# Second causal attention: exponentials turned in 32x32 squares on VectorE and moved through DRAM, instead of turned 128x128 on TensorE

## The chip, the core and the metric

The kernel runs on one core of one Trainium2 chip. A core has a matrix engine (TensorE, PE in the profile, with its weight loads as PEld), three engines for elementwise work (VectorE = DVE, ScalarE = ACT, GpSimd = POOL), and queues that start transfers (SP's queue carries nearly all of them here). Each engine works through its own instructions in order and waits on semaphores for the others. The metric is the device time of one execution in microseconds (us): the median of several runs, 882.38 us before the change.

## What is computed

The reference is a decoder of two layers on 8 sequences of 128 tokens with 512 features, in float32. Each layer is a self attention, a second attention over a context, and a feed-forward part; each part is added to the residual and normalized over the features. The change lies in the second layer's self attention:

```python
qkv = jnp.clip(jnp.einsum('bsd,ed->bse', hidden_states, Wqkv), -8, 8)
q, k, v = jnp.split(qkv, [512, 1024], axis=-1)
q = _layer_norm(q, q_ln_w, q_ln_b); k = _layer_norm(k, k_ln_w, k_ln_b)
# 32 heads of 16 features
scores = jnp.einsum('bqhd,bkhd->bhqk', q, k) * scale + slopes * (key_pos - query_pos)
scores = jnp.where(causal, scores, -1e30)
probs = jax.nn.softmax(scores, axis=-1)
out = jnp.einsum('bhqk,bkhd->bqhd', probs, v)          # then @ Wout, + x, layer norm
```

## The kernel before

**The stage.** The second layer's self attention is a loop over 8 batches (sequences), `for b in range(B)`, and in it over `f in (0, 2)`: two units of 16 heads each, 16 units in all. I name a unit by (b, f) and call f = 0 the even and f = 2 the odd unit. Around the loop's units run the projections of the next batch and the output projection of the last one:

- even unit: scores of the unit, then `normed(0, b + 1)` (queries of the next batch: four matmuls, clip to +-8, layer norm over rows) and `normed(1, b + 1)` (keys, the same, and on POOL a product with and a sum of the norm's weights, L669 and L670);
- odd unit: scores of the unit, `turned_queries` (the next queries are turned by TensorE, L691, and copied with scale and bias by ACT), `values`, `turned_tokens` of batch b + 2, `projection` of batch b - 1 (8 matmul records, in two halves), and `turned_keys` (the keys turned by TensorE, L701, and multiplied by DVE into `kbd`, two copies with the other head of each pair zeroed, L703).

**A unit (class Heads16).** TensorE writes the scores into two double banks of PSUM (L165; the pool of double banks, `ps2`, has two). DVE adds the bias, negates and takes the row minimum, head by head: 16 instructions of L184 that write the tile `e` (two buffers). ACT takes the exponential in place with the row sum (`exps`, L197), 16 instructions. `divide` takes the reciprocals (DVE, L208) and multiplies the exponentials (POOL, L211). `turn` has TensorE turn `e` in twelve 128x128 transposes (L228) through the same double banks, and DVE and ACT each copy half of the result to SBUF as `pT` (L229). `out` multiplies the turned probabilities with the values (L247, L253), and DVE copies the result into `oT` (L259). A unit is turned in the following unit and its `out` is made in the one after that.

**What sets the order.** Instructions are recorded in program order, and a scheduler may move them; a few places pin it with `tc.issue_after`. `late` and `keys_late` hold norms that are pushed behind the heads of the next unit. Single banks of PSUM (`ps1`, four) are handed out in turn to the projections, the turned pieces and `out`. After the loop come pieces of the following attention (`front.go`), whose weights `w_X_...` are loaded on SP's queue while this stage runs.

**The helper of the norms.** `moments` is three instructions on DVE (statistics L91, aggregate L93, variance plus epsilon L95) and a power on POOL (L97); the row norm itself is one instruction of DVE (L107, L667).

Of the kernel before, what the change touches and what calls it, by code (L numbers as in the profile page):

```python
# [13 lines left out]
ALU = mybir.AluOpType  # L14
# [29 lines left out]
def decoder(ctx: ExitStack, tc: tile.TileContext, a: dict, out: bass.AP):  # L44
# [69 lines left out]

    late = []
# [30 lines left out]
    class Heads16:  # L146
# [11 lines left out]
        def __init__(self, pool, units, bias, o_dst, name, between=()):  # L158
            self.pool, self.units, self.o_dst, self.name, self.rc = pool, units, o_dst, name, None
            s = [banks(f"s_{name}_{i}") for i in range(2)]  # L160
# [9 lines left out]
            self.e = pool.tile([P, 4, self.W], F32, tag="e", name=f"e_{name}", bufs=2)  # L170
            self.m = sm.tile([P, 2, 4, 2], F32, tag="m", name=f"m_{name}")
            self.su = sm.tile([P, 2, 4, 2], F32, tag="su_a", name=f"su_{name}")
            for i in range(2):
                if i and between:
                    while between:
                        with tc.issue_after(self.scored.ins):
                            self.scored = between.pop(0)()
                with tc.issue_after(self.scored.ins) if i else nullcontext():
                    for part in range(2):
                        for r in (2 * i, 2 * i + 1):  # L180
                            for x in range(2):
                                w = P >> part
                                cols = slice(2 * P * part + w * x, 2 * P * part + w * x + w)
                                self.scored = nc.vector.tensor_tensor_reduce(  # L184
                                    self.e[:, r, cols], s[i][:, r % 2, cols], bias(r, cols), -1.0, 3e38,
                                    ALU.add, ALU.min, self.m[:, part, r, x : x + 1],
                                )
# [4 lines left out]
        def exps(self, half):  # L192
            for part in range(2):
                e = self.by_heads(part)
                for r in (2 * half, 2 * half + 1):
                    for x in range(2):
                        nc.scalar.activation(  # L197
                            e[:, r, x, :], e[:, r, x, :], AF.Exp, scale=-1.0,
# [13 lines left out]

        def turn(self):


            if self.rc is None:
# [3 lines left out]
                rb = self.pool.tile([P, 2, 8, HD], F32, tag="rb", name=f"rb_{self.name}", bufs=1)  # L220
                nc.gpsimd.tensor_copy(rb, bc(rc.rearrange("p (a h) -> p a h", a=2).unsqueeze(3), [P, 2, 8, HD]))
            self.pT = self.pool.tile([P, 4, self.W], F32, tag="pT", name=f"pT_{self.name}", bufs=1)
# [14 lines left out]
            self.rT = self.pool.tile([P, 2, P], F32, tag="rT", name=f"rT_{self.name}", bufs=1)  # L237
            nc.scalar.copy(self.rT, pr[:, : 2 * P].rearrange("p (a q) -> p a q", a=2))

        def out(self):  # L240
            o = bank(f"o_{self.name}")
            for u, (_, _, v, vd) in enumerate(self.units):
                v, vd = (t() if callable(t) else t for t in (v, vd))
                late = slice(u * P + 64, u * P + P)
                for x in range(2):
                    for r in range(4):
# [3 lines left out]
                            rhs=self.pT[:, r, x * P + 64 * u : x * P + 64 * u + 64], start=(x == 0), stop=(x == 1),  # L250
                        )
                for r in range(4):
# [3 lines left out]
                        rhs=self.pT[:, r, 2 * P + 64 * u : 2 * P + 64 * u + 64], start=True, stop=True,  # L256
                    )
            if self.rc is not None:
# [7 lines left out]
            )  # L266

# [25 lines left out]
    idle = ap.tile([P, 4, 3 * P], F32, tag="e", name="idle").rearrange("p r k -> p (r k)")[:, :512]  # L293
# [355 lines left out]
    v_bufs = [values_tiles(qp, i) for i in range(2)]  # L649
# [6 lines left out]
    def normed(i, b, xT, later=None):  # L656


        n, w = (("q", w1q), ("k", w1k))[i]
        pq = bank(f"p{n}1_{b}")  # L660
        mm_acc(pq, [(xT[:, c, :], w[:, c, :]) for c in range(NC)])
        q = qp.tile([P, D], F32, tag=n, name=f"{n}1_{b}")
        nc.vector.tensor_scalar(q, pq, 8.0, -8.0, ALU.min, ALU.max)
        mean, rs = moments(q, f"{n}1_{b}")

        def normalized():
# [180 lines left out]
    for b in range(B):  # L847
# [3 lines left out]
        for f in (0, 2):  # L851
# [11 lines left out]
            if turned:  # L863
                turned.out()
# [533 lines left out]
```

## Time and profile before

| what | value |
|---|---|
| median of the runs shown | 882.38 us (880.0 to 883.82) |
| the profiled execution's own time | 883.9 us |
| its span | 882.1 us |
| granted TensorE clock, mean | 0.994 |
| busy: PE, DVE, ACT, POOL | 853.1, 545.8, 369.3, 188.5 us |
| first score matmul of the stage | at 325.30 us |
| first matmul after the stage's last projection | at 510.31 us |
| first heads instruction of unit (1,0), (7,0), (7,2) | at 349.10, 482.75, 490.19 us |
| one steady batch (two units) | 22.14 us |

How to read the profile: one execution is recorded, and every instruction has a start, a duration and what it waited for. A group names line, engine, operation, output and inputs, how often, busy time, mean duration in ns, and the idle time of its engine just before it with what ended that. The windows view gives busy time by engine in a stretch of time. The chain is the work that ended last, followed back from the end of the program, or, between two times, in order of time. The timeline lists the instructions by start. Instructions of one engine overlap a little: the start of the next one comes before the end of the last, so a chain of them is priced here from start to start.

### The profile page before, as it was taken

What the parts mean: (1) busy time and instruction counts of PE and PEld (TensorE: products, weight loads), DVE (VectorE), ACT (ScalarE), POOL (GpSimd) and SP (SyncE); (2) the same over time, 40 slices, a digit from 0 to 9 for tenths busy, and PEclk for the clock granted to TensorE, in tenths of its full rate; (3) what the DMA queues carried; (4) which work ended last, traced back from release to release, by engine and by line L of the source; (5) the groups of instructions that cost most, each with busy time, mean ns of one, the idle gap of its engine ahead of it and who ended that gap; (6) DMA issues with size and microseconds to landing.
All of it is one profiled execution on the core that took longest, in us unless ns stands there. A gap on an engine that the chain in (4) does not pass through costs nothing.

```text
span 882.1 us, 17898 instructions
## 1 busy us (share of the span) xinstructions
PE 853.1 (97%) x6482; PEld 529.9 (60%) x6482; DVE 545.8 (62%) x2166; ACT 369.3 (42%) x1535; POOL 188.5 (21%) x267
## 2 busy tenths in 40 slices
PE   9999999999899999999999999999999999999996
PEld 5766655655455455555555687758475846576454
DVE  3656787777869567777778622735363545467654
ACT  3877564754222136666666503213122322224310
POOL 2500223133333314555555300000000000000000
PEclk9999999999999999999999999999999999999999
DMA  8700000130300002000004010331213211313340
GB/s 327 306 2 26 1 14 13 49 108 1 144 13 24 1 1 97 2 1 2 2 2 145 27 72 1 75 88 42 48 37 85 44 47 37 83 43 76 81 97 36
DMA packets 30073, 50.73 MB, mean 58 GB/s; under 512 B 5536, under 2 KB 22048, under 8 KB 28192
## 3 DMA queue, kind: packets, MB, share of 16 engines
q1 hardware_dynamic: 27424, 47.49, 17.9%
q10 hardware_dynamic: 2560, 2.10, 1.1%
q8 instruction: 51, 0.84, 0.4%
q14 instruction: 38, 0.31, 0.1%
HBM read 30.69 MB, written 2.10 MB: 37 GB/s over the span
## 4 chain that ended last, share of the span: by engine, by line
PE 72%; DVE 17%; ACT 6%; POOL 2%; issue 1%; DMA 1%; SPq 0%; ACTq 0%; POOLq 0%; DVEq 0%
PE pqx L86 9%; PE pox L994 7%; PE pv L86 5%; PE pkx L86 4%; PE pvx L86 4%; PE s_x L932 4%; PE o_x L977 4%; PE pq L86 4%; PE pk L86 3%; PE po L711 3%; ACT e_a L197 3%; DVE e_a L184 3%; PE pt_a L228 3%; PE pof L618 2%; PE s_a L165 2%; PE po L86 2%
## 5 line engine op out<-in xcount | busy, mean ns | idle before, releaser
L197 ACT ACTIVATE e_a<-e_a,m_a 128x128 f32<-128x128 f32 (+1 forms) x512 | 184.8, 365 | 100.2 <-DVE m_a L184 100.2
L953 ACT ACTIVATE e_x<-s_x,m_x 128x256 f32<-128x256 f32 x128 | 58.6, 483 | 140.0 <-DVE m_x L943 132.1
L197 ACT ACTIVATION_READ_ACCUMULATOR e_a<-e_a,m_a 128x1 f32 x512 | 97.6, 191 | 0.0
L86 PE MATMUL pqx<-xTx,w_X_q 128*128 128x256 f32 x384 | 84.9, 380 | 0.0
L86 PEld LDWEIGHTS pqx<-xTx,w_X_q 128*128 128x128 f32 x384 | 72.6, 190 | 11.4 <-issue 1.8
L994 PE MATMUL pox<-w_X_o,oTx 128*128 128x512 f32 x168 | 74.1, 596 | 0.7 <-DVE oTx L983 0.6
L942 DVE TENSOR_REDUCE m_x<-s_x 128x4 f32<-128x1024 f32 x32 | 37.6, 1218 | 41.2 <-PE s_x L932 41.2
L97 POOL TENSOR_TENSOR rs_x<-ve_x,neghalf 128x1 f32<-128x1 f32 x7 | 3.8, 548 | 268.8 <-DVE ve_x L95 249.8
L211 POOL TENSOR_TENSOR e_a<-e_a,rc_a 128x512 f32<-128x512 f32 (+1 forms) x64 | 52.7, 845 | 34.9 <-DVE rc_a L208 19.3
L994 PEld LDWEIGHTS pox<-w_X_o,oTx 128*128 128x128 f32 x168 | 31.3, 190 | 40.9 <-issue 39.2
L932 PE MATMUL s_x<-kTx,qTx 32*128 32x256 f32 x768 | 50.0, 385 | 1.2 <-ACT e_x L953 1.1
L228 PE MATMUL pt_a<-ident,e_a 128*128 128x128 f32 x384 | 48.0, 273 | 2.7 <-DVE m_a L184 2.7
L228 PEld LDWEIGHTS pt_a<-ident,e_a 128*128 128x128 f32 x384 | 43.6, 140 | 11.1 <-issue 5.0
L184 DVE CUSTOM_DVE_ANT_0 e_a<-s_a,masks 128x128 f32<-128x128 f32 (+1 forms) x256 | 47.1, 252 | 4.5 <-PE s_a L165 3.2
L932 PEld LDWEIGHTS s_x<-kTx,qTx 32*128 32x128 f32 x768 | 39.0, 184 | 17.4 <-issue 11.7
L184 DVE CUSTOM_DVE_ANT_0 e_a<-s_a,alibi 128x128 f32<-128x128 f32 (+1 forms) x256 | 47.4, 253 | 2.2 <-PE s_a L165 1.3
L977 PE MATMUL o_x<-pT_x,vx 128*32 128x512 f32 x384 | 43.7, 595 | 1.9 <-issue 0.7
L184 DVE DVE_READ_ACCUMULATOR2_ANT m_a<- 128x1 f32 x512 | 42.4, 83 | 0.1
L961 DVE STREAM_TRANSPOSE e_x<-e_x 128x1024 f32<-128x1024 f32 x32 | 39.7, 1241 | 0.8
L960 DVE TENSOR_SCALAR e_x<-e_x,rc_x 128x256 f32<-128x256 f32 x128 | 36.3, 347 | 3.9 <-DVE rc_x L957 2.2
L165 PEld LDWEIGHTS s_a<-kbd,qT 32*64 32x64 f32 x1024 | 20.7, 131 | 28.5 <-issue 15.4
L103 DVE TENSOR_TENSOR x_x<-pox,x_a 128x512 f32<-128x512 f32 x7 | 4.8, 686 | 52.5 <-PE pox L994 52.5
(236 smaller groups left out, 1627.1 us busy)
## 6 DMA issues: line engine op xcount, KB each, us to landing
pT_x<-e_x SPq DMA_DIRECT2D x224, 64.0 KB, 2.0
w_X_q<-in_X_q SPq DMA_DIRECT2D x3, 1024.0 KB, 4.8
w_X_o<-in_X_o SPq DMA_DIRECT2D x3, 1024.0 KB, 4.7
w_L_Wv<-in_L_Wv SPq DMA_DIRECT2D x2, 1024.0 KB, 7.3
w_L_Wo<-in_L_Wo SPq DMA_DIRECT2D x2, 1024.0 KB, 8.0
x_in<-in_x SPq DMA_DIRECT2D x8, 256.0 KB, 8.5
ct<-in_ctx SPq DMA_DIRECT2D x8, 256.0 KB, 2.6
cT<-in_ctxT SPq DMA_DIRECT2D x4, 512.0 KB, 3.8
```

What stands on the lines that cost most here:

```text
L86: nc.tensor.matmul(ps, lhsT=l, rhs=r, start=(i == 0), stop=(i == n - 1))
L165: nc.tensor.matmul(s[r // 2][64 * u : 64 * u + 64, r % 2, cols], lhsT=qT[rows, 64 - 64 * part : P - 64 * part], rhs=kbd[rows, :, :keys], s ...
L184: self.scored = nc.vector.tensor_tensor_reduce(self.e[:, r, cols], s[i][:, r % 2, cols], bias(r, cols), -1.0, 3e38, ALU.add, ALU.min, self ...
L197: nc.scalar.activation(e[:, r, x, :], e[:, r, x, :], AF.Exp, scale=-1.0, bias=self.m[:, part, r, x : x + 1], accum_out=self.su[:, part, r, ...
L211: nc.gpsimd.tensor_tensor(e, e, bc(self.rc[:, part, rs, :].unsqueeze(3), list(e.shape)), ALU.mult)
L228: nc.tensor.transpose(pt[:, r, cols], self.e[:, 2 * i + r, cols], ident)
L932: nc.tensor.matmul(sc[g // 2][:, g % 2, u * 256 : (u + 1) * 256], lhsT=qT[rows, (h0 + u) * NS + n, :], rhs=kT[rows, n], start=(n == 0), st ...
L942: nc.vector.tensor_reduce(m, self.s[i], AX.X, ALU.max, negate=True)
L953: nc.scalar.activation(self.e[:, :, j, :], self.s[half][:, i, :].rearrange("p (a k) -> p a k", k=32), AF.Exp, bias=self.m[:, j : j + 1], s ...
L961: nc.vector.transpose(self.e[:, :, js, :], self.e[:, :, js, :])
L977: nc.tensor.matmul(po[32 * g : 32 * g + 32, :], lhsT=v[:, s, g * XD + 32 * n : g * XD + 32 * n + 32], rhs=pT[:, s].rearrange("p i h x -> p ...
L994: nc.tensor.matmul(po, lhsT=oT[:, n, h * P : (h + 1) * P], rhs=w, start=(i == 0), stop=(i == NX - 1))
```

## The change

Fifteen of the 16 units become `Squares16`; only the last, (7, 2), stays `Heads16`. What it does, part by part:

1. **The turn.** `Squares16` writes `e` in another layout: 14 rows of 32 for each of 4 groups of keys, twelve rows of exponentials and two rows for the reciprocals of the sums. `move` takes the reciprocals (DVE), has POOL spread them into the two rows (`tensor_copy`, 128x256), has DVE transpose 32x32 squares in place (two instructions, 128x1536 and 128x256 elements), stores the whole tile to a buffer in DRAM (`kept`, one DMA of 128 rows of 7168 bytes, 896 KB), and loads it back as `pT` in four DMAs of 224 KB, each with 32 partitions and rows of 1792 bytes, so that the groups change places with the partitions. `turn` and `divide` of these units are empty: the probabilities are divided after `out`, by a product with the turned reciprocals (`divided`). No transposes on TensorE, no copies from PSUM and no products on POOL remain for them.
2. **Depth.** A unit is moved in the following unit and its `out` is made three units after its scores (`pending`), instead of two. `pT` has two buffers, `e` two as before, `kept` three, `v` three, `oT` three. The output projection is made two batches late instead of one, and so one projection more stands after the loop.
3. **The keys' copies.** `kbd` is written by two instructions of ACT (`nc.scalar.mul`, 128x512 each) instead of one of DVE.
4. **The norms.** Clip and statistics (`moments`) and the row norm (`norm`) of queries and keys are placed one by one: queries' clip, statistics and norm before the odd unit's heads, keys' clip and statistics between the two halves of the odd unit's heads, keys' norm behind them. The norm after the residual (`late_norms`) stands around the even unit's `move`. `chosen_experts(B - 1)` normalizes at once.
5. **The order.** From the loop's start to its drain, `in_order` ties every instruction of TensorE, VectorE and ScalarE to the one before it on its engine, so that these three keep the program's order. POOL and SP are left to the scheduler.
6. **Elsewhere.** In `Heads16` (the first layer's attention uses it too) the reciprocals' tile `rb` becomes the tail of `e` and `rT` the tail of `pT`. Four pieces of the following attention are made in the last batch and one in the drain, as before.

Where the built program puts what matters below: DVE in the even unit has the 16 heads, `divided` of the unit three before, statistics of the residual, the reciprocals and two transposes of `move`, the residual's norm, then queries' clip, statistics and norm; in the odd unit half of the heads, keys' clip and statistics, the other heads, keys' norm, `divided`, reciprocals and transposes, values' clip, the residual's sum. POOL in the odd unit has the keys' two products (L669 and L670 of before), then the copy of the reciprocals, then the copies of the values. The first heads instruction of each unit from (1,0) on carries a wait for the store to `kept` of the unit two before it, whose buffer of `e` it takes.

```diff
-            self.e = pool.tile([P, 4, self.W], F32, tag="e", name=f"e_{name}", bufs=2)
+            self.begin()
...
+    class Squares16(Heads16):
+        def begin(self):
+            self.tile = self.pool.tile([P, 4, 14, 32], F32, tag="e", name=f"e_{self.name}", bufs=2)
+            self.e = self.tile[:, :, :12, :].rearrange("p g (r t) k -> p r t g k", r=4)
...
+        def move(self):
+            rc = sm.tile([P, 16], F32, tag="rc", name=f"rc_{self.name}")
+            nc.vector.reciprocal(rc, self.sums.rearrange("p r a x -> p (r a x)"))
+            nc.gpsimd.tensor_copy(
+                self.tile[:, :, 12:14, :].rearrange("p g a (x d) -> p g (a x) d", x=2),
+                bc(rc.rearrange("p (r h) -> p r h", r=4).unsqueeze(3), [P, 4, 4, HD]),
+            )
+            for rows in (slice(0, 12), slice(12, 14)):
+                nc.vector.transpose(self.tile[:, :, rows, :], self.tile[:, :, rows, :])
+            kept = kept_rows.tile([P, 4, 14 * 32], F32, tag="kept", name=f"kept_{self.name}")
+            nc.sync.dma_start(kept, self.tile.rearrange("p g r k -> p g (r k)"))
+            self.pT = self.pool.tile([P, 4, 14, 32], F32, tag="pT", name=f"pT_{self.name}", bufs=self.places)
+            by_group = kept.rearrange("(i k) g x -> k i g x", i=4)
+            to = self.pT.rearrange("p i r k -> p i (r k)")
+            for g in range(4):
+                nc.sync.dma_start(to[32 * g : 32 * g + 32], by_group[:, :, g, :])
+        def turn(self):
+            pass
+        def divide(self, half, behind=None):
+            pass
+        def divided(self, o):
+            by_half = "p u (a i q) -> p a u i q"
+            rT = self.pT[:, :, 12:14, :].rearrange("p (u i) a q -> p a u i q", u=2)
+            nc.vector.tensor_tensor(
+                self.o_dst.rearrange(by_half, a=2, i=2),
+                o[:, : 2 * P].rearrange("p (u t) -> p u t", u=2).rearrange(by_half, a=2, i=2),
+                rT[:, ::-1],
+                ALU.mult,
+            )
...
         kbd = ap.tile([P, 2, D], F32, tag="kbd", name=f"kbd1_{b}")
-        turned_keys.done = nc.vector.tensor_tensor(kbd, bc(pt.unsqueeze(1), [P, 2, D]), bc(pair.unsqueeze(2), [P, 2, D]), ALU.mult)
+        for x in range(2):
+            nc.scalar.mul(kbd[:, x, :], pt, pair[:, x : x + 1])
...
+    attn_order.enter_context(in_order(nc.tensor.engine, nc.vector.engine, nc.scalar.engine))
     for b in range(B):
...
+            if f and more:
+                q.norm()
+            kind = Heads16 if (b, f) == (B - 1, 2) else Squares16
+            now = kind(
+                ap, units, alibi_bias(f), oT[:, f : f + 2, :], f"a1_{b}_{f}", [k.moments] if f and more else [], places=2
+            )
             now.exps(0)
+            if f and more:
+                k.norm()
+            if len(pending) == 3:
+                pending.pop(0).out()
+            if f and more:
+                qT = turned_queries(b + 1, q)
+            now.divide(0)
+            now.exps(1)
+            now.divide(1)
+            if f == 0:
+                if more:
+                    q = Normed(0, b + 1, xT)
+                normalize = late_norms()
+                if prev:
+                    prev.move()
+                normalize()
+                if more:
+                    q.moments()
...
+                if more:
+                    k = Normed(1, b + 1, xT)
+            else:
+                prev.move()
+                if more:
+                    v = values(b + 1, xT)
...
+                half = projection(b - 2, oTs.pop(b - 2)) if b > 1 else iter((0, 0))
+                next(half)
...
+                if more:
+                    qk = qT, turned_keys(b + 1, k)
+                next(half)
+            pending.append(now)
+            prev = now
+    normalize = late_norms()
+    pending[0].out()
+    normalize()
+    list(projection(B - 2, oTs[B - 2]))
+    prev.turn()
+    pending[1].out()
...
+    prev.out()
+    list(projection(B - 1, oTs[B - 1]))
```

## The prediction

> **What bounds the kernel now.** I read the page first, then the stretches of one batch each, then the chain of one batch in order of time, then the prices of single instructions. The page:
>
> ```profile
> PE 853.1 (97%) x6482; PEld 529.9 (60%) x6482; DVE 545.8 (62%) x2166; ACT 369.3 (42%) x1535; POOL 188.5 (21%) x267
> PE 72%; DVE 17%; ACT 6%; POOL 2%; issue 1%; DMA 1%; SPq 0%; ACTq 0%; POOLq 0%; DVEq 0%
> ```
>
> TensorE is busy for 97% of the span and carries 72% of the chain. In the stage of the change (185.0 us, from 325.30 to 510.31) this holds batch by batch; columns are the stretch, its length, then busy us of PE, PEld, DVE, ACT, POOL, the granted clock and the DMA share:
>
> ```profile
> 371.52:393.66 22.14, 21.57 (x229) 12.29 (x228) 17.46 (x89) 14.92 (x71) 11.34 (x15) 1.00 0.01 2
> 393.66:415.80 22.14, 21.57 (x229) 12.30 (x228) 17.45 (x89) 14.93 (x71) 11.46 (x15) 1.00 0.01 2
> ```
>
> A batch takes 22.14 us, of which PE is idle for 0.57. DVE has 4.7 us of air by this count, and the DMA engines do nothing. The chain inside a batch, in order of time:
>
> ```profile
> 446.56 1.04 POOL e_a L211
> 447.60 0.52 POOL rs_q L97
> 448.14 1.26 DVE q L667
> 449.45 0.66 PE pTq L691 x4
> ...
> 454.98 1.31 PE pt_a L228 x12
> 456.29 1.72 PE po L711 x4
> 458.01 0.44 PE pTk L701 x4
> ```
>
> Here are the idle 0.57 (L691 waits for the queries' norm, itself queued behind a POOL product) and the twelve transposes of one unit, 1.31 us of PE.
>
> **What goes.** Fifteen units lose 1.31 us of PE each, 19.7 us in all; ACT and DVE lose a copy each and POOL its products. Were PE still the bound, a batch would be 22.14 - 0.57 - 2.62 = 18.95 us. So the question is what is late next. Two things are: a longer program on DVE, and a new ring that runs through a transfer.
>
> **The ring.** `e` has two buffers. The first heads instruction of a unit waits until the store of the unit two before it has landed, and that store is issued only when DVE has turned that unit, one unit later. So from first heads to first heads a unit takes at least: DVE from its heads to the end of the squares, plus the store. Prices, from the DVE timeline (start, duration), the groups and the transfers:
>
> ```profile
> 394.61 0.29 DVE L184 CUSTOM_DVE_ANT_0 e_a<-s_a,alibi 128x128 f32<-128x128 f32 x1
> ...
> 397.46 0.69 DVE L91 BATCH_NORM_STATS2 st_a<-x_a 128x6 f32<-128x512 f32 x1
> 398.06 0.41 DVE L259 COPY oT<-o_a 128x256 f32<-128x256 f32 x1
> 398.39 0.17 DVE L93 BATCH_NORM_AGGREGATE mv_a<-st_a 128x2 f32<-128x6 f32 x1
> ```
>
> ```profile
> L961 DVE STREAM_TRANSPOSE e_x<-e_x 128x1024 f32<-128x1024 f32 x32 | 39.7, 1241 | 0.8
> ```
>
> ```profile
> L670 POOL TENSOR_TENSOR k<-k,lnv 128x512 f32<-128x512 f32 x7 | 8.9, 1273 | 0.5
> L669 POOL TENSOR_TENSOR k<-k,lnv 128x512 f32<-128x512 f32 x7 | 8.9, 1268 | 9.5 <-DVE k L667 9.5
> ```
>
> ```profile
> w_X_q<-in_X_q SPq DMA_DIRECT2D x3, 1024.0 KB, 4.8
> ct<-in_ctx SPq DMA_DIRECT2D x8, 256.0 KB, 2.6
> out<-x_f SPq DMA_DIRECT2D x7, 256.0 KB, 2.2
> out<-x_before SPq DMA_DIRECT2D x1, 256.0 KB, 2.0
> ```
>
> Even unit: sixteen heads 2.85 (394.61 to 397.46; same elements, in runs of 32, taken at the same price), `divided` 0.33 (the L259 copy from start to start, as long), the residual's statistics 1.01 (keys' L91 starts at 405.74, their L95 ends its turn at 406.75), reciprocals 0.17, squares 2.17 (1792 elements at 1241 ns per 1024; POOL's copy of the reciprocals, 0.40 by the first layer's row L221, is hidden by the first of the two). Sum 6.53.
>
> Odd unit: heads 2.85, keys' clip 0.60 and statistics 1.01 between them, keys' norm 0.54. Then POOL is next: its queue has the two products L669 and L670 (2.62 with the gap between them) ahead of the copy of the reciprocals (0.40), and the second transpose (0.45) waits for that. `divided`, reciprocals and the big transpose (2.2 us) lie beside it. With two hops between the engines of 0.09 each (POOL's L97 starts 0.08 behind DVE's L95) the sum is 8.65.
>
> The store: 896 KB. No row shows one. From the loads, 2.6 us at 256 KB and 4.8 at 1024 KB give 4.43; from the store of 256 KB (2.0) with the same slope, 3.83. I take 4.1, the middle, since the direction is that of the second row and the size that of the first. Bounds: 3.65 (2.0 and 640 KB at the 397 GB/s that the two last stores reach), 4.8 (the full 1024 KB row). Hops on SP and back 0.1. So even to odd is 10.73 us, odd to even 12.85: a batch of **23.6 us** against 22.14. DVE's own program (18.3 us by these prices), PE's 18.95 and ACT's (14.92, minus two copies of 0.79, plus two of 0.58) fit into it, and idle.
>
> The Trainium skill has a rule that speaks against the store: "DMA: Bandwidth & Descriptors", section "Anatomy of one DMA", says that a transfer signals only once its last byte is confirmed, and that the confirmation is slowest when HBM is written. The rows here show the opposite sign, 2.0 to 2.2 us for a store and 2.6 for a load of the same size. By the rule the store would take 4.43 or more and the sum grow by some 5 us; an estimate by that page's fit for another queue (2.0 us plus bytes at 436 GB/s) is 4.1.
>
> **What lies beside.** The loads back (4 times 224 KB) start when the store lands and take some 4.5 us (four issues at 0.33 to 0.6 us, as SP's other issues take, and the 4.1 of as many bytes, mostly overlapped); they are wanted two units later, about 20 us after the squares. That covers 9 us of transfer twice over; without that cover `out` would wait for all of it. `kbd` on ACT takes 1.2 us (two at 577 ns, the L139 copy) instead of 1.22 on DVE: it ends some 10.0 us after the odd unit's first heads, and with 0.9 of scores behind it the next heads could start at 10.9, 2 us before the ring lets them. The queries' norm costs 0.55 instead of 1.25, since POOL's products beside it are gone; it runs while the store travels. Four weights of 1 MB and one block of 528 KB share SP's queue with the stage; they are issued behind a store, so I count nothing, with a bound of 5 us if each delays a store by its own 2.7 us of bytes half the time. The first layer's new tiles only add waits that its order meets anyway: nothing, within 1 us.
>
> **Sum.** Up to unit (0,2) nothing waits on the ring; its heads start at 337.7 as before, so unit (1,0)'s start at 337.7 + 8.65 + 4.2 = 350.55, before 349.10: +1.45. Batches 1 and 2 have no residual norm yet (22.6 each), batches 3 to 6 take 23.6: 139.6 against 482.75 - 349.10 = 133.65: +5.95. Unit (7,0): 10.73 against 490.19 - 482.75 = 7.44: +3.3. The drain from (7,2)'s heads: squares of (7,0) end at 5.5, stored at 9.75, loaded at 15.6, then on PE `out` 0.8, a front piece 2.6, `out` 0.8 with 0.45 of DVE, projection 3.3: 23.6 against 510.31 - 490.19 = 20.1: +3.5. Together +14.2 on the profiled execution's 883.9 us, 898.1. That execution lies 1.5 above the median of 882.38, so the median should be **897 us**.
>
> **Rivals.**
> - *The store is quick (ends faster).* Every 0.1 us of the store is worth 1.4 us (14 waits). At 3.1 us the sum is zero; below about 2.6 the ring no longer binds: then DVE's even unit (6.53 and residual norm 0.47, queries' clip and statistics 1.6, POOL's power 0.65, norm 0.46: 9.7) and the odd unit's way from keys' norm over POOL, PE and ACT to the next scores (10.9) give 20.6 a batch and about 876 us. For it: stores beat loads by 0.4 to 0.6 us here. Against: 256 KB alone take 2.0, so 640 KB more would have to go at over 1000 GB/s.
> - *No change to speak of.* A store of 3.65 and POOL products at 1.04 (the L211 form) take 6.3 and 3.5 us off: about 887; a bit more of the same lands at 882.
> - *Traffic (slower).* A store in company takes 5.4 us and more (the 768 KB load of `w_X_k` did), or squares cost more in the strided layout: 14 times 1.3 is 18 more, 915 us.
> - *PE's clock falls.* The granted clock was 1.00 in nearly all stretches; now PE idles for 23.6 - 18.95 = 4.65 us a batch, at the queries' and at the keys' turn. The Trainium skill, "TensorE: Matmul & The Clock Gate", section "What's actually happening", lets the clock drop to half after an idle window of about 3.4 us. By it a wait of 4.7 in one piece could halve one window, 1.7 us of work that the same wait covers, so nothing is added.
>
> **How the numbers follow.** Forecast (883 to 906) 0.66, quick store 0.12, no change 0.08, traffic 0.14. The range of 880 to 909 leaves out most of the quick store and half of the traffic. A change of 0.5% (4.4 us) is about what this measurement can tell. Faster 0.13, same 0.09, slower 0.78.
>
> **What would show it.** Heads instructions idle before a unit on the transfer of `kept`, some 2.2 us in front of even and 1.0 in front of odd units, 20 us and more in all; `kept` landing 4.1 us after issue; batches of 23.6 from batch 3 on; PE waiting for DVE at the queries' turn and for POOL at the keys' turn, its busy time 20 us less; the second transpose of the odd unit waiting for POOL. Wrong if `kept` lands in under 3.1 us, if heads wait for PE instead, or if a batch is bound by DVE without idle time.

## The result

The changed kernel takes **908.18 us** (906.81 to 910.55) where the kernel before took 882.88 us beside it (880.0 to 883.82): a ratio of 1.0295, interval 1.0263 to 1.0328, 26 us slower. The forecast was 897 us within 880 to 909: slower as said, and by the cause that was said, but only 14.2 of the 26 us were in the sum. The time lies 0.8 us inside the upper edge of the range. That upper part was meant for stores in traffic or dear squares; most of what fills it is the drain, so that the range held is in part luck. The ratios here and below leave out two executions of a slower state, 903.16 us of the kernel before and 3005.75 of the last kernel.

The profile after, from its page: busy times and shares of the chain.

```profile
PE 848.1 (93%) x6302; PEld 518.2 (57%) x6302; DVE 549.1 (60%) x2158; ACT 369.1 (41%) x1536; POOL 145.8 (16%) x224
PE 60%; DVE 17%; DMA 8%; ACT 7%; POOL 3%; issue 2%; SPq 1%; ACTq 1%; POOLq 0%; DVEq 0%
```

TensorE has 180 matmuls fewer, yet it is busy only 5 us less, because the others run at a lower clock; it carries 60% of the chain, not 72%, and a new carrier has come in, the DMA with 8%. Two batches, by stretches from first heads to first heads (length, then PE, PEld, DVE, ACT, POOL, granted clock, DMA share):

```profile
422.61:447.26 24.65, 19.87 (x203) 9.84 (x202) 17.79 (x89) 14.79 (x71) 5.66 (x9) 0.93 0.50 151
447.26:470.12 22.86, 20.64 (x205) 10.40 (x204) 17.86 (x89) 14.79 (x71) 5.66 (x9) 0.93 0.55 163
```

A batch took 22.14 us before. These two take 24.65 and 22.86, batches 1 to 7 take 22.3 to 25.0, and no engine fills them: in the two, PE idles for 2.2 to 4.8 us, DVE for 5 to 7. What DVE waits for stands in the groups (busy, mean ns, idle before, and what ended that), and the store with the median time from issue to landing:

```profile
L222 DVE CUSTOM_DVE_ANT_0 e_a<-s_a,alibi 128x128 f32<-128x128 f32 (+1 forms) x256 | 47.5, 253 | 31.8 <-DMA kept_a<-e_a 25.3
L345 DVE STREAM_TRANSPOSE e_a<-e_a 128x1536 f32<-128x1536 f32 (+1 forms) x30 | 31.5, 1071 | 6.0 <-POOL e_a L340 6.0
...
kept_a<-e_a SPq DMA_DIRECT2D x15, 896.0 KB, 4.5
```

The heads wait 25.3 us for the store, and the odd unit's second transpose waits for POOL. Both were in the forecast. The chain of one batch in order of time (start, duration) has the ring in full:

```profile
427.05 1.97 DVE e_a L345 x2
429.06 5.48 DMA kept_a<-e_a
...
439.88 1.27 POOL k L780
441.23 1.26 POOL k L781
442.49 0.35 POOL e_a L340
442.86 0.46 DVE e_a L345
443.37 3.72 DMA kept_a<-e_a
```

First heads of the even unit stand at 422.61 and its squares end at 429.00 by DVE's timeline: 6.39 us, forecast 6.53. The odd unit starts at 434.68 and ends its squares at 443.31: 8.63, forecast 8.65. The two stores behind them took 5.48 and 3.72, though, where 4.1 was in the sum.

Where the 26.6 us between the two profiled executions lie (908.7 - 882.1 of span), by first heads and first matmuls:

| stretch | before | after | more | forecast |
|---|---|---|---|---|
| up to the first heads of (0,0) | 327.04 | 328.97 | +1.9 | 0 |
| (0,0) to (1,0) | 22.06 | 25.23 | +3.2 | +1.45 |
| batches 1 to 6 | 133.65 | 140.95 | +7.3 | +5.95 |
| (7,0) to (7,2) | 7.44 | 11.74 | +4.3 | +3.3 |
| drain, from (7,2) | 20.1 | 30.46 | +10.3 | +3.5 |
| the rest | 371.8 | 371.4 | -0.4 | 0 |

The first row I put down to the execution, the longest of four (910.55), and not to the change: four kernels below (p1, t1, d1, d2) have the same instructions up to there, and their first score matmul of the stage starts at 322.3 to 323.5 us (before: 322.66, changed: 324.40). The drain alone is out by 6.9. So two things had to be tested: that the ring, not the order or TensorE, is what sets the batches, and what fills the drain.

### The profile page after: what moved, and what is told of

Same layout as the page of the kernel before. It is cut to its first block, busy times and chain, and to the rows that moved or that the text cites. A ratio compares the mean times of both kernels' runs of the same rounds, so it can differ in the third digit from the quotient of the medians.

```text
span 908.7 us, 17674 instructions
## 1 busy us (share of the span) xinstructions
PE 848.1 (93%) x6302; PEld 518.2 (57%) x6302; DVE 549.1 (60%) x2158; ACT 369.1 (41%) x1536; POOL 145.8 (16%) x224
## 4 chain that ended last, share of the span: by engine, by line
PE 60%; DVE 17%; DMA 8%; ACT 7%; POOL 3%; issue 2%; SPq 1%; ACTq 1%; POOLq 0%; DVEq 0%
PE pqx L86 9%; DMA kept_a<-e_a 6%; PE pox L1135 6%; DVE e_a L222 4%; ACT e_a L235 4%; PE pvx L86 4%; PE pq L86 4%; PE s_x L1073 4%; PE o_x L1118 4%; PE pkx L86 3%; PE pk L86 3%; PE pv L86 3%; PE pof L725 2%; PE s_a L184 2%; PE po L86 2%
## 5 line engine op out<-in xcount | busy, mean ns | idle before, releaser
L222 DVE CUSTOM_DVE_ANT_0 e_a<-s_a,alibi 128x128 f32<-128x128 f32 (+1 forms) x256 | 47.5, 253 | 31.8 <-DMA kept_a<-e_a 25.3
L964 ACT COPY qTx<-pqx 128x512 f32<-128x512 f32 x24 | 14.1, 593 | 63.4 <-PE pqx L86 63.4
L184 PE MATMUL s_a<-kbd,qT 32*64 32x256 f32 (+1 forms) x1024 | 35.0, 353 | 4.6 <-ACT kbd L815 2.7
L345 DVE STREAM_TRANSPOSE e_a<-e_a 128x1536 f32<-128x1536 f32 (+1 forms) x30 | 31.5, 1071 | 6.0 <-POOL e_a L340 6.0
```

The costliest lines, as they stand in the source:

```text
L184: nc.tensor.matmul(s[r // 2][64 * u : 64 * u + 64, r % 2, cols], lhsT=qT[rows, 64 - 64 * part : P - 64 * part], rhs=kbd[rows, :, :keys], s ...
L222: self.scored = nc.vector.tensor_tensor_reduce(self.block(part, r, x), self.alike(s[:, cols]), self.alike(bias(r, cols)), -1.0, 3e38, ALU. ...
L345: nc.vector.transpose(self.tile[:, :, rows, :], self.tile[:, :, rows, :])
```

## The experiments

The kernel before ran beside each of them on the same chip. The last column is the ratio's distance from one times 882.9 us.

| run | median us | ratio to before | interval | us |
|---|---|---|---|---|
| the change | 908.18 | 1.0295 | 1.0263 to 1.0328 | +26.0 |
| e1_three_e | 886.21 | 1.0044 | 1.0024 to 1.0063 | +3.9 |
| o1_order_alone | 930.61 | 1.0546 | 1.0524 to 1.0568 | +48.2 |
| u1_no_order | 916.27 | 1.0391 | 1.0369 to 1.0412 | +34.5 |
| p1_pool_first | 903.09 | 1.0240 | 1.0217 to 1.0263 | +21.2 |
| t1_weights_late | 904.51 | 1.0261 | 1.0241 to 1.0281 | +23.0 |
| d1_drain | 908.66 | 1.0302 | 1.0275 to 1.0329 | +26.7 |
| d2_squares_first | 904.42 | 1.0235 | 1.0209 to 1.0262 | +20.7 |
| s1_keys_first | 889.97 | 1.0097 | 1.0063 to 1.0131 | +8.6 |
| s2_keys_first_weights_late | 889.82 | 1.0091 | 1.0076 to 1.0107 | +8.0 |
| f1_three_e_filled | 887.41 | 1.0055 | 1.0034 to 1.0076 | +4.9 |
| f2_keys_first_later_turn | 881.80 | 0.9983 | 0.9968 to 0.9999 | -1.5 |
| f3_turns_and_drain | 874.02 | 0.9899 | 0.9870 to 0.9928 | -8.9 |

**The ring: a third buffer.** The theory is that the heads wait for the store because `e` has two buffers. The wait can't be taken away alone, but a third buffer takes away what makes it:

```diff
-            self.e, self.behind = self.rows("e", 2)
+            self.e, self.behind = self.rows("e", self.places + 1)
...
-            self.tile = self.pool.tile([P, 4, 14, 32], F32, tag="e", name=f"e_{self.name}", bufs=2)
+            self.tile = self.pool.tile([P, 4, 14, 32], F32, tag="e", name=f"e_{self.name}", bufs=3)
...
-        kbd = ap.tile([P, 2, D], F32, tag="kbd", name=f"kbd1_{b}")
+        kbd = ap.tile([P, 2, D], F32, tag="kbd", name=f"kbd1_{b}", bufs=1)
```

> The changed kernel with three buffers of e instead of two (and one of kbd instead of two, to make room). Nothing else moves; the heads of a unit no longer wait for the store of the unit two before. Ring theory: the heads' idle time on the transfer of kept (31.8 us) goes, batches fall from 22.3 to 25.2 us to about 20.6 (even unit 9.7 by DVE, odd unit 10.9 by the way of the keys), unit (7,0) from 11.7 to about 10; the drain stays at 30. About 22 us less than the changed kernel's 908.2: 886, within 4. Rival 1, traffic or the longer program of DVE is the bound: the waits move to the loads of pT or to DVE, batches stay above 22.5, 900 or more. Rival 2, TensorE's clock is the cost: batches go to about 20.6 but the clock stays under 0.95 in them and 895 to 900 comes out.

It came out at 886.21. The group of the heads and one batch by stretches:

```profile
L222 DVE CUSTOM_DVE_ANT_0 e_a<-s_a,alibi 128x128 f32<-128x128 f32 (+1 forms) x256 | 47.4, 252 | 11.3 <-PE s_a L184 10.6
```

```profile
423.26:444.05 20.79, 19.21 (x204) 9.64 (x204) 17.69 (x89) 14.80 (x71) 5.66 (x9) 1.00 0.59 179
```

No wait for `kept` is left. A steady batch takes 20.79 us, an even unit 9.68 and an odd one 11.12; the forecast's rival of the quick store had worked out 20.6, 9.7 and 10.9 for a batch without the ring. The granted clock is back at 1.00 without anything done for it, so in the batches the low clock followed from the ring's waits; TensorE doesn't appear in the chain of the batch above. The ring is shown: 22 of the 26 us go with it. What remains against before is the drain (28.07 against 20.1): there TensorE stands 4.6 us before the output of (6,0), whose load of `pT` took 6.27 us from issue to landing, beside a weight and then a store. Batches 1 to 6 take 126.7 us, where they took 133.65 before and 140.95 in the change: without the ring the squares do gain 7 us there, and the drain eats them up.

**The order alone.** All units turned by TensorE, in the changed loop:

```diff
-            kind = Heads16 if (b, f) == (B - 1, 2) else Squares16
+            kind = Heads16
...
-                prev.move()
+                prev.turn()
```

> The order alone: every unit is turned by TensorE as before the change (twelve transposes, two copies), but in the changed kernel's loop: depth of three units, order of TensorE, VectorE and ScalarE written out, kbd by ScalarE, projection two batches late. No squares, nothing moved through DRAM. Theory that the squares' way through DRAM is the whole loss: about the time of before, 883 to 890. Rival, the written order itself costs most of it (each engine stands where the scheduler had moved something forward): 900 or more. Second rival, the order is worth something by itself: under 879.

The rival was right, and by far: 930.6 us. Batches take 25.3 to 29.2 us. TensorE's waits in the stage (line, releaser, us in all, times, longest):

```profile
PE pt_a L269 <- DVE m_a L222: 24.0, 18, 2.3
PE pTq L801 <- DVE q L778: 6.4, 5, 1.5
```

The transposes need the double banks of the scores, so they wait until the next unit's heads have read them; in the written order everything else of TensorE stands behind them, and the clock falls on top (0.50 from 450.0 to 452.5, after waits of 0.85 and 2.31). So this loop suits only a turn that leaves TensorE alone. The forecast set no price on it at all. The changed loop has more in it than the order (the depth, the places of the norms, the keys' copies on ScalarE); which part of the 48 us is the order's own, no run shows. Against this kernel, with the same loop, the squares are worth 22 us.

**The change without the order.**

```diff
-    attn_order.enter_context(in_order(nc.tensor.engine, nc.vector.engine, nc.scalar.engine))
```

> The changed kernel without the written order: TensorE, VectorE and ScalarE are left to the scheduler as before the change, all else as changed. Ring theory: the two buffers of e and the store bind whatever the order, so 900 to 915. Rival, the written order is itself a cost (the order alone, with the units turned by TensorE, came out at 930.6 against 882.7): under 895. Second rival, the order is what makes the squares bearable, since a scheduler that does not know the transfers puts the squares behind later heads: over 920.

916.27, 1.3 us above what was expected, and not by the expected way. The group of the heads:

```profile
L222 DVE CUSTOM_DVE_ANT_0 e_a<-s_a,alibi 128x128 f32<-128x128 f32 (+1 forms) x256 | 47.3, 252 | 3.9 <-PE s_a L184 3.7
```

There is no wait for the store. The scheduler puts the squares of (3,0) ahead of the heads of (3,2), so the buffer comes free early, but DVE then stands behind ScalarE's exponentials of the same unit: in the chain 5.83 us of exponentials, the reciprocals, the squares, TensorE's output projection and the residual's norm follow each other up to the next heads. The ring is gone and a longer chain is in its place; first heads follow each other by 8 to 19 us. The written order is worth some 8 us to the change.

**POOL's queue.** The keys' two products pinned behind the copy of the reciprocals:

```diff
+                    with tc.issue_after(prev.spread.ins):
+                        k.weigh()
```

(`weigh` is the two products taken out of `norm`, `spread` the copy.)

> The changed kernel with the keys' two products on POOL pinned behind the copy of the reciprocals, so that in an odd unit the copy does not queue behind them. Ring theory with the odd segment bound by POOL's queue: the odd unit's squares end about 1.0 us earlier in seven units (8.66 to about 7.6, then bound by keys' norm, divided, reciprocals and the large transpose of 1.72 on DVE), the keys' products end 0.4 later, which the wait for the store covers: 6 to 7 us less than 908.2, 901.5. Rival, the keys' turn on TensorE is what sets the batch: 0 or slower by the 0.4 times 7.

903.09, some 5 us less, where 6.7 were expected. The group of the heads:

```profile
L222 DVE CUSTOM_DVE_ANT_0 e_a<-s_a,alibi 128x128 f32<-128x128 f32 (+1 forms) x256 | 47.5, 252 | 24.6 <-DMA kept_a<-e_a 13.5 <-PE s_a L184 10.1 <-issue 0.2
```

The second transpose's wait for POOL falls from 6.0 us to 0.3, and the heads' wait for `kept` from 25.3 to 13.5; instead they wait 10.1 for the scores. An odd unit takes 11.95 us where it took some 12.6: there it is the keys' way that ends last, through POOL, TensorE and the scores. Its products end 8.65 us after the first heads instead of 7.81: 0.4 of that is the copy put ahead, the rest `divided` and the reciprocals, for which the copy itself waits. The step in the forecast, that the copy stands behind the two products, is shown.

**The weights.** The loads for the next attention issued behind the last load of `pT` (`loaded` is that load):

```diff
-    for k in ("q0", "q1", "q2"):
-        wqs.append(weight4(f"X_{k}"))
-    wos = [weight(f"X_o{i}").rearrange("p (c o) -> p c o", c=4) for i in range(3)]
+    with tc.issue_after(Heads16.loaded.ins):
+        for k in ("q0", "q1", "q2"):
+            wqs.append(weight4(f"X_{k}"))
+        wos = [weight(f"X_o{i}").rearrange("p (c o) -> p c o", c=4) for i in range(3)]
```

> The changed kernel with the loads of the next attention's weights (w_X_q, w_X_o) issued behind the last load of pT, not inside the stage. Nothing else moves. Theory that these loads slow the stores and loads beside them: the first store falls from 7.2 to about 3.6 us and batch 0 by about 3.5, three stores and three groups of loads from batch 6 on by about 1 us each, some 6 us in all: 902 against 908.2; no store takes over 5.6. Rival, they cost nothing, as predicted: 908 within 1.5. Upper limit: if they delay the queries of the next attention, more than 908.

904.51; the interval of the ratio overlaps that of the change, so 3 us is a likely size and no more. The trace is plainer. The transfers of this run, and behind them the two issues on SP's queue in the change that the first store is about (start, duration):

```profile
kept_a<-e_a SPq DMA_DIRECT2D x15, 896.0 KB, 3.7
```

```profile
345.69 0.33 SPq L67 DMA_DIRECT2D w_X_q<-in_X_q  x1
346.87 0.33 SPq L347 DMA_DIRECT2D kept_a<-e_a  x1
```

The first store takes 3.48 us instead of 7.20, and the first batch 22.27 instead of 25.23. In the change the weight was issued 1.2 us ahead of that store, not behind it: the store's first packet started 3.49 us after its issue (0.84 in a store by itself), and its packets (7168 bytes) then took 272 ns each, as in a store by itself. So this store stood behind the weight. Four others, (5,2), (6,0), (6,2) and (7,0), had a weight or the block of 528 KB issued 0.4 us behind them: their later packets took up to 521 ns, and three of them landed in 4.5 us instead of 3.6, that of (6,2) in 5.13.

The expected 6 us were twice what came. No store took over 5.6, as expected, but the gain from batch 6 on stayed out: the store of (6,2) took 5.43, now with no weight beside it, and that of (7,0) 4.51, still with the 528 KB beside it. Stores of 4.76 and 5.42 remain at (3,0) and (3,2), too, with no weight. There the packets tell: in the change a packet of 16 KB of the instructions' queue was under way while the packets of (0,2), (3,0) and (3,2) were starting, and these stores took 4.55, 4.83 and 5.48, the last packets landing one by one. Where such a packet started 3.1 us after the issue or later, when the store's last packet had started already, the stores took 3.56 to 3.72. Over all runs, 18 stores with such a packet under way and no other transfer took 4.20 to 5.74 us, and 101 with neither took 3.47 to 4.29. In the kernel without the order, where every second store took some 4.8, it was loads of `pT` that ran beside them.

**The drain, first try.** The last two units turned by TensorE:

```diff
-            kind = Heads16 if (b, f) == (B - 1, 2) else Squares16
+            kind = Heads16 if 2 * b + f // 2 >= 2 * B - 2 else Squares16
...
                 prev.move()
+                prev.turn()
```

> The changed kernel with the last two units (7,0) and (7,2) turned by TensorE, not only (7,2). Theory that the drain's extra 10 us are the store and load of (7,0) with nothing beside them, and TensorE's clock after two waits of nearly 4 us: the drain falls from 30.5 to about 22 to 23, 7 to 8 us less than 908.2, about 901, and the granted clock in the drain stays near 1.00. Rival, the drain is long because one projection more stands in it and PE's order is written out: less than 2 us gained.

Nothing gained, 908.66. The drain falls by 2.0 (28.45), but (7,0) to (7,2) grows from 11.74 to 14.34. DVE's timeline says why (idle before, and its releaser, in brackets):

```profile
498.80 0.20 DVE L246 RECIPROCAL rc_a<-su_a 128x8 f32<-128x8 f32 x1 [2.66 <-ACT e_a L235]
...
506.80 0.29 DVE L222 CUSTOM_DVE_ANT_0 e_a<-s_a,alibi 128x128 f32<-128x128 f32 x1 [3.82 <-DMA kept_a<-e_a]
```

A unit turned by TensorE takes its reciprocals in its own unit, and they wait for ScalarE. In the written order the squares of the unit before, (6,2), stand behind them; so their store goes out later, and the next heads wait for it. The same pair stands in the drain of the change itself, where (7,2) is such a unit. That gave the next run.

**The drain, second try.** One move in DVE's order:

```diff
+            if f and not more:
+                prev.move()
             now.divide(0)
             now.exps(1)
             now.divide(1)
...
-                prev.move()
                 if more:
+                    prev.move()
```

> The changed kernel with one move in VectorE's written order: in the last odd unit the squares of (7,0) stand ahead of the reciprocals of (7,2), which wait for ScalarE's exponentials (2.66 us in the changed kernel) and send POOL products that the copy of (7,0)'s reciprocals queues behind (0.9). Theory that the drain is a chain of latencies from the last heads over squares, store, load and output: the store of (7,0) is issued about 5.7 us after the first heads of (7,2), not 9.1, and the drain falls by 3.6, to 26.9: 904.5. Rival, the drain is TensorE's work at a low clock (or the loads' traffic): less than 1 us gained.

904.42 against the expected 904.5; that it agrees to 0.1 is luck, since the drain fell by 6.4 where 3.6 was expected. The store of (7,0) is issued 5.45 us after the first heads of (7,2), where it was 9.12, and the drain takes 24.08 us, not 30.46. For comparison the drain of the change, from its chain:

```profile
513.52 1.61 POOL e_a L249 x2
515.13 0.35 POOL e_a L340
515.50 0.46 DVE e_a L345
...
516.01 4.51 DMA kept_a<-e_a
...
521.89 4.63 DMA pT_a<-kept_a
...
528.07 5.01 PE pvx L86 x8
```

The reader sees the products of (7,2) ahead of the copy of (7,0)'s reciprocals, the store, the load, and then eight matmuls that take 5.01 us; in the run with the squares first they take 2.78:

```profile
523.03 2.78 PE pvx L86 x8
```

So of the 6.4 us, 3.7 are the store's earlier issue and 2.2 are the clock, which did not fall behind this wait, now 1.78 us and not 3.91 (it did behind the one before, of 3.28). Between the two profiled executions 5.8 us are left of the 6.4, as unit (7,0) took 0.9 longer and the rest balances to 0.3.

**Towards a better kernel.** With the ring gone, the odd unit is bound by the keys' way. So queries and keys change places: the keys are projected in the even unit, normalized ahead of the odd unit's heads, and POOL's products run beside the heads; the queries take the place between and behind the heads.

```diff
-                q.norm()
+                k.norm()
...
-                ap, units, alibi_bias(f), oT[:, f : f + 2, :], f"a1_{b}_{f}", [k.moments] if f and more else [], places=2
+                ap, units, alibi_bias(f), oT[:, f : f + 2, :], f"a1_{b}_{f}", [q.moments] if f and more else [], places=2
...
-                k.norm()
+                q.norm()
...
-                qT = turned_queries(b + 1, q)
+                kbd = turned_keys(b + 1, k)
...
-                    qk = qT, turned_keys(b + 1, k)
+                    qk = turned_queries(b + 1, q), kbd
```

> Three buffers of e (one of kbd), and queries and keys change places: the keys of the next batch are projected and normalized in the even unit, the queries in the odd unit. Theory that with the ring gone the odd unit is set by the way of the keys (norm, two products on POOL, TensorE, ScalarE, scores: 11.1 us), and that the products are hidden when they run under the odd unit's heads: batches fall from 20.8 to about 19.2 (TensorE's own work is 18.95 by the prediction's count), 10 us less than the 886.2 with three buffers alone: 875 within 3. Rival, VectorE's program or ScalarE is the bound, batches stay at 20.5 or more: 884 or more.

> The kernel with three buffers and the keys first, and the next attention's weights issued behind the last load of pT besides. Theory that the drain of the kernel with three buffers waits for a load of pT that lands 6.3 us after its issue beside a weight (481.2 to 485.8 on TensorE), and runs at a low clock after it: that wait goes, the first batch falls by about 2, some 5 to 7 us less than keys first alone: 868 within 4. Rival, the drain is set by TensorE's work (one projection and two outputs more in it): less than 2 us.

Neither gained on three buffers alone: 889.97 and 889.82. From batch 3 on the odd unit takes 12.1 to 15.1 us, where it took 11.12. In the second of them, TensorE's timeline:

```profile
445.75 0.66 PE L812 MATMUL pTk<-ident,k 128*128 128x128 f32 x4 [3.03 <-POOL k L781]
446.24 5.30 PE L86 MATMUL pv<-w_L_Wv,xTa 128*128 128x512 f32 x8
```

In the written order TensorE stands before the keys until POOL is done, and then the values' matmuls run at a low clock (0.60 from 445.75 to 448.50): the wait costs its 3.03 us and 1.6 more. The weights' share could not be told behind this.

The next two runs keep three buffers and late weights. The first has queries first; its norm of the residual stands behind the queries' statistics, and the squares of (7,0) stand first as above. The second exchanges queries and keys again, and turns the keys behind the values and tokens.

```diff
-                normalize()
                 if more:
                     q.moments()
+                normalize()
```

```diff
                     if b + 2 < B:
                         xT = turned_tokens(b + 2)
...
+                if more:
+                    kbd = turned_keys(b + 1, k)
                 half = projection(b - 2, oTs.pop(b - 2)) if b > 1 else iter((0, 0))
```

> Three buffers of e (one of kbd), the next attention's weights issued behind the last load of pT, the squares of (7,0) ahead of the reciprocals of (7,2), and one exchange on VectorE in the even unit: the queries' clip and statistics stand ahead of the residual's norm, so that this norm (0.47) fills the wait for POOL's power (0.65). From 886.2 with three buffers alone: the exchange 6 times 0.45 = 2.7, the weights 2 to 4, the drain 0 to 3.6: 879, within 4. Steady even unit 9.2, odd unit 11.1. Rival, the gains do not add, because the drain was covered by TensorE's own work once the ring was gone: 883.

> As the kernel before this one, with queries and keys exchanged once more, but the keys turned by TensorE behind the values and the turned tokens, so that TensorE does not stand 3.0 us before POOL's products and its clock stays up (in keys first the values' eight matmuls took 5.13 us after that wait instead of 3.5). Theory that this wait alone spoiled keys first: even unit 9.2, odd unit about 10.5 (TensorE's own work in it), batches 19.7: about 3.5 us less than the kernel before this one, 875, within 4. Rival, ScalarE then sets the odd unit (exponentials, tokens, keys, queries in a row): odd unit 11.5 or more, 880 or more.

The first gave 887.41, no gain on three buffers alone. The even unit fell by 0.2, to 9.46 and not to 9.2, and the drain grew to 30.8: a load of the feed-forward's weights (`wf`) now stood ahead of the loads of `pT` of (6,2) on SP, and the store of (7,0) took 8.57 us among them. The second gave 881.80, with an odd unit of 11.45: TensorE waits 0.98 and 0.71 for single banks that DVE releases (after the queries' norm, and after the values' clip behind the squares). That is a point for the rival in size, not in cause, since it is DVE's order that holds TensorE up. The last run moves those two, and fills the drain; its stores are also issued behind the loads of the unit before, and the block `wf` with its bias behind all loads:

```diff
-            if f and more:
-                q.norm()
-            if len(pending) == 3:
-                pending.pop(0).out()
             if f and not more:
                 prev.move()
+                front.go(2)
+            if len(pending) == 3:
+                pending.pop(0).out()
+            if f and more:
+                q.norm()
...
                 if more:
-                    prev.move()
                     v = values(b + 1, xT)
+                    prev.move()
...
-                else:
-                    front.go(2)
...
     prev.turn()
+    front.go(1)
     pending[1].out()
     normalize = late_norms()
     normalize()
-    front.go(1)
```

> As keys first with the later turn, and: in the odd unit the outputs' product stands ahead of the queries' norm and the values' clip ahead of the squares on VectorE, so that TensorE no longer waits for two single banks that these release (0.98 before the projection, 0.71 before the queries' turn, every odd unit); in the last unit the squares of (7,0) and two pieces of the next attention stand ahead of the output of (6,0) (TensorE stood 3.66 us there for a load of pT), and one more piece ahead of the output of (7,0) (2.27); stores stand behind the loads of the unit before, and the loads of the next attention's last weights behind all of these. Theory that what is left are these waits and the low clock behind them: odd unit 10.0 instead of 11.45 (TensorE's own work in it), 5 times 1.4 = 7; the drain 5 to 8 shorter: 881.8 - 13 = 869, within 5. Rival, ScalarE or VectorE take the waits over: 877 or more.

874.02, ratio 0.9899 (0.9870 to 0.9928): faster than both kernels, and at the very edge of the 864 to 874 that were expected. Several things changed at once here, and no run tells their shares. Two batches by stretches:

```profile
417.70:437.22 19.52, 18.99 (x208) 9.77 (x205) 17.60 (x89) 14.81 (x71) 5.95 (x9) 1.00 0.64 190
437.22:456.74 19.52, 18.74 (x197) 9.57 (x197) 17.59 (x89) 14.80 (x71) 5.95 (x9) 1.00 0.65 189
```

A batch takes 19.52 us, 0.5 to 0.8 more than TensorE's busy time in it, and the forecast's count of TensorE's own work was 18.95. The odd unit takes 10.06, the drain 26.6. In the drain a wait of 3.00 for the load of (6,2) is left, and the matmuls behind it are slow again.

## Why the prediction was right, and where not

- **What bounds.** Right. The ring over `e` and the store sets the batches: with a third buffer 22 of the 26 us go, and the heads no longer wait.
- **DVE's segments.** Right to 0.15 us in the steady batches: 6.39 and 8.63 for 6.53 and 8.65, POOL's queue among them, as the run with the copy first confirmed.
- **The store, taken at 4.1, bounds 3.65 to 4.8.** The middle was fair for the sum, but no single size was right. Of the 14 stores that are waited for, seven took 3.50 to 3.73 and seven 4.49 to 7.20, on average 4.40: 0.3 more than the term, some 4 us of the sum by an estimate from these numbers. By itself a store takes 3.5 to 3.7, at or under the lower bound drawn from the rate of small stores; in company it takes 4.5 to 7.2. The Trainium skill, "DMA: Bandwidth & Descriptors", section "Anatomy of one DMA", says that the confirmation is slowest when HBM is written, and from that and the loads here the forecast had worked out 4.43 or more: the stores by themselves stay below it, and the average comes near it only by the company.
- **Weights, counted at nothing.** Wrong. The step says "they are issued behind a store". One of them was issued 1.2 us ahead of the first store, which took 7.20 instead of 3.48 for it: that is nearly the whole of the +3.2 in the first batch. Others were issued 0.4 us behind a store and still cost it some 0.9 us each. About 3 us in all, inside the bound of 5.
- **Up to (0,2), nothing.** The heads of (0,2) do not start "at 337.7 as before": in the profile before they start at 338.86, and 337.7 is where the scores of that unit end on TensorE. The number came right all the same, 337.6 when the 1.9 us of the later start are taken off its 339.52, because the keys' statistics no longer stand ahead of these heads; that is luck.
- **The drain, +3.5.** Wrong, +10.3, the largest miss. The failed step is "squares of (7,0) end at 5.5": they end 9.06 us after the heads of (7,2) and the store is issued at 9.12, because the reciprocals of (7,2) wait for ScalarE ahead of them in DVE's written order. DVE's timelines before and after show this wait:

```profile
497.14 0.20 DVE L208 RECIPROCAL rc_a<-su_a 128x8 f32<-128x8 f32 x1 [1.64 <-ACT e_a L197]
```

```profile
513.24 0.20 DVE L246 RECIPROCAL rc_a<-su_a 128x8 f32<-128x8 f32 x1 [2.66 <-ACT e_a L235]
```

So it stood in the profile of before, 6.95 us after the heads of (7,2), but no squares stood behind it there: the step priced the work and not the queue in which it stands. Of the 6.9 us that the term lacked, 3.6 are this, 0.4 the store and the loads, and 2.9 TensorE's work behind them, most of it the clock. With the one move in DVE's order the drain takes 24.08 against the forecast's 23.6.
- **One sign failed.** TensorE's busy time was to fall by 20 us and fell by 5 (853.1 to 848.1), since the other matmuls ran at a lower clock. The other signs came.
- **The clock, "nothing is added".** Right in the batches: the ring's segments hold at a granted clock of 0.93, and three buffers bring it back to 1.00. Wrong in the drain, where nothing covers it: eight matmuls took 5.01 us instead of 2.78. The Trainium skill, "TensorE: Matmul & The Clock Gate", "What's actually happening", lets the clock fall after an idle window of about 3.4 us; the drain's waits of 3.59 and 3.91 agree, though shorter ones did it too (below).
- **The order.** Not priced at all. With the squares it is worth 8 us, by the run without it; the whole changed loop without squares costs 48.
- **Before the stage, nothing.** Right, as far as one execution each shows: the +1.9 there is the spread between executions.

## What to carry to other kernels

When work leaves the engine that bounds, follow each buffer that it touches round its ring: from its first write to the last reader, a transfer included. The third buffer was worth 22 us here, more than any single move of an instruction. When an order is written out by hand, price every instruction by what stands ahead of it on its engine or queue, the last loop pass above all, where one kind of unit follows another; most of the drain's miss, and what went wrong in d1, s1 and f1, was of that kind. And look at what a transfer is issued beside: a weight issued 1.2 us ahead of a store held its packets back by 2.7 us, and one issued 0.4 us behind a store slowed its later packets from 272 to 521 ns.

## What the runs showed of the hardware

- A store of 896 KB to HBM takes 3.5 to 3.7 us when it runs alone (t1, and the undisturbed stores of the change); a load of 1024 KB took 4.8 before. With a weight issued on the same queue 1.2 us ahead it took 7.20, at 272 ns a packet; with one issued 0.4 us behind, its later packets took up to 521 ns and it landed in some 4.5.
- A packet of 16 KB of the instructions' queue, under way while a store's packets start, goes with a late store: 4.20 to 5.74 us in 18 such stores, 3.47 to 4.29 in 101 without one (all runs, no other transfer beside them). That it is the cause is argued from the packets' times; no run took the instructions' packets away.
- Where TensorE's granted clock is low, it is 0.5 in stretches of 3.41 us or a multiple (433.54 to 436.95 and 525.70 to 532.53 in the change). Short waits can be enough: after 2.28 us with almost no matmul (494.6 to 496.9 in f2) it was 0.67 on average for the next 5.3 us, and after 3.05 us (s2) it was 0.60. The length of a wait alone does not settle it: in the change one of 1.90 us before 457.17 lowered the clock, and one of 1.89 before 408.69 did not.
